# A gated graph network and a batch-normed one: z ahead of the high part, x's load on ScalarE's queue, and row sums of one adjacency on ScalarE

## The chip, the cores and the metric

The kernel runs on one core of a Trainium2 chip. The time is the device time of one execution in microseconds, and lower is better. A comparison of two kernels rests on several executions of each on the same chip. The engines are named as in the profile: PE multiplies matrices (PEld loads its weights), DVE is the vector engine, ACT the scalar engine, POOL the general one (GpSimd), and SP issues most of the transfers. Each engine works through its own instructions in order.

## The reference

There are 16 graphs of 1024 nodes with 128 features, and a dense adjacency of 1024 x 1024 for each, of zeros and ones. The first part runs four gated steps on the normalised features of each graph:

```python
h = relu(layernorm(x))
for i in range(4):
    m  = einsum('bjn,bjd->bnd', adj, h @ weight[i])
    r  = sigmoid(m @ w_ih_r.T + h @ w_hh_r.T + b_r)
    z  = sigmoid(m @ w_ih_z.T + h @ w_hh_z.T + b_z)
    n  = tanh(m @ w_ih_n.T + b_in + r * (h @ w_hh_n.T + b_hn))
    h  = (1 - z) * n + z * h
x = x + h * mask
```

The second part runs four graph convolutions with a batch norm over all graphs and nodes after each:

```python
h = relu(layernorm(x))
for i in range(4):
    h = relu(einsum('bnm,bmc->bnc', adj, h @ W[i]) + b[i])
    h = gamma[i] * (h - mean(h)) * rsqrt(var(h) + 1e-5) + beta[i]
out = x + h
```

## The kernel before, in words

The function that runs is exact_path. It keeps features transposed, 128 features on the partitions and nodes along the row, in two halves of 512 nodes. For the big product with the adjacency the features are split into a high part, which is the value rounded to the short float type fp32r, and a low part, which is what is left. Each adjacency goes through eight row tiles of 128 x 1024, so one aggregation is 8 rows x 2 parts x 2 halves = 32 products of 128x512, all at line 524. Both parts are cast on chip: ACT writes the high part (line 925, method high), DVE subtracts for the low part (line 932, method low).

In the gated part two streams run against each other, sa with the even graphs and sb with the odd ones. A half step (function half_step) puts the gates of one stream, called two, beside the preparation and the aggregation of the other, called one. A counter, clock, begins at 3 and counts them: two first steps, then 60 half steps. The gates of a half are six products at line 999 (method products; each is two PE instructions of 128x512), into four banks named g_r, g_hn, g_xn and g_z. The second half's products use the same four banks, so each of them waits until the first half's reader of that bank is done: the sigmoids at lines 1017 (reset_gate) and 1026 (update_gate, for z) on ACT, and two DVE operations at lines 1018 and 1019. Then come tanh (line 1022, candidate), h minus candidate (line 1035, less), the product with z (line 1039) and the sum with the candidate (line 1040), the last two both in method mixed.

The new h reaches the other layout by way of memory. DVE transposes blocks of it (line 720), SP writes it to cross_h (line 591) and reads it back as n_h (line 598), from which high and low are made one half step later. The aggregation of stream one, which follows the gates on PE, needs high and low of the first half when it starts and those of the second half midway. When it ends, ACT copies its two banks to m (line 961), and the next half step's products begin.

The order of all this is written out by hand for every engine (manual_schedule). Work that recurs only in some half steps is put in an agenda: at(n, place, go) asks that go be issued in half step n at a place such as "start", "beside0", "beside1", "mid", "gap" or "late", and due(place) issues it. A stream's method plan, called with n when the stream begins a graph, puts there the norm of the graph that it finished (sums in "gap" of n+2, stores of xmid and ymid by POOL in "mid", y_mid blocks on ACT in n+4) and the preparation of the graph that it takes next: the load of its x (next_load, line 539, on POOL's queue, "late" of n+4), its sums on DVE, its factors, and its blocks on ACT. For adjacencies, POOL also casts rows to bf16 (line 615), SP transposes them by DMA, and POOL stores the turned adjacency of 2 MB to memory (line 629) for the second part. While a stream is at its last gates, its next adjacency is fetched to stage tiles, rounded on POOL (line 577), and inspected by ACT (glance, line 586), which reads a row tile of 128x1024 into a junk tile and adds it up per partition.

The second part is ordered by a planner, on ACT and DVE from the last gates on. For each graph it loads the turned adjacency (line 1319), casts it to fp32r on DVE and ACT (lines 1324 and 1322), and aggregates. At layer 0 the features come ready from memory (first_split, lines 1379 to 1382, tiles y and chw), and the weights are applied after (first_weights, lines 1391 and 1392). The first graph of later layers is aggregated before its batch norm is known, and raw_weights (line 1409) corrects it with degree, the sums of the first adjacency for each node, kept alike on all partitions. Function row_sums makes them: sixteen products of 128x512 with a matrix of ones (line 1418), and two copies on ACT (line 1422), after the first graph's aggregation of layer 0. PE's order there is the planner's too: they come out in the middle of the second graph's products. degree shares its room with w_mT, the gates' weights, which are then no longer used.

Of the kernel before, what the change touches and what calls it, by code (L numbers as in the profile page):

```python
# [8 lines left out]
F32 = mybir.dt.float32  # L9
# [7 lines left out]
P = 128  # L17
# [324 lines left out]
def exact_path(  # L342
# [39 lines left out]
    def tmp(name):  # L382
        return ps_t.tile([P, HALF], F32, tag="tmp", name=name)

    adjT_d = [dram.tile([NB, P, N], BF16, tag=f"adjT{b}", name=f"adjT_d{b}") for b in range(B)]
    xmid_d = [dram.tile([N, C], F32, tag=f"xmid{b}", name=f"xmid_d{b}") for b in range(B)]
    ymid_d = [dram.tile([P, N], F32, tag=f"ymid{b}", name=f"ymid_d{b}") for b in range(B)]
# [20 lines left out]
    nc.vector.memset(eps_t, EPS)  # L408
    ones = const.tile([P, 1], F32, tag="ones", name="ones")
    nc.vector.memset(ones, 1.0)  # L410
    low = const.tile([P, (B + 2) * NB], F32, tag="low", name="low")
    nc.vector.memset(low, 0.0)

# [119 lines left out]
    with ExitStack() as st:  # L533
# [46 lines left out]
        def glance(b, stage, js):  # L580

            junk = work.tile([P, N], BF16, tag="junk", name=f"junk{b}_{js[0]}", bufs=1)
            for j in js:
                lows = stage[j % 4].bitcast(U16).rearrange("p (n t) -> p n t", t=2)[:, :, 0]
                k = b * NB + j
                nc.scalar.activation(junk, lows, AF.Copy, accum_out=low[:, k : k + 1])

        def exchange_out(t, name, d=None):
            if d is None:
# [180 lines left out]
        class Stream:  # L770
# [35 lines left out]
                norm_blocks(self.xt, self.y, self.norm, ks)  # L806

            def next_load(self):
                self.next_x = load_x(self.b + 2, nc.gpsimd)

            def next_sums(self):
                self.next_norm = norm_stats(self.next_x, f"in{self.b + 2}")
# [12 lines left out]
            def plan(self, n, tail=None):  # L825

                if tail:
                    b, xt, hT, parts = tail
                    end = {}

                    def sums():
                        end["norm"] = tail_sums(b, xt, hT, parts)

                    def blocks(hf):
                        if hf == 0:
                            end["y"] = y_mid(b)
                        norm_blocks(xt, end["y"], end["norm"], range(hf * BH, (hf + 1) * BH))

                    at(n + 2, "gap", sums)
                    at(n + 3, "mid", lambda: store_xmid(b, xt))  # L840
                    at(n + 3, "gap", lambda: norm_factors(end["norm"]))
                    at(n + 4, "beside0", lambda: blocks(0))
                    at(n + 4, "beside1", lambda: blocks(1))
                    at(n + 5, "mid", lambda: store_ymid(b, end["y"]))
                if self.b + 2 < B:
                    at(n + 4, "late", self.next_load)
                    at(n + 6, "start", self.next_sums)
                    at(n + 6, "gap", self.next_factors)
# [123 lines left out]
            def gate_step(self, hf, between=None):  # L972
                self.products(hf)
                self.reset_gate(hf)
                if between:
                    between()
                self.candidate(hf)
                self.update_gate(hf)
                self.less(hf)
                self.mixed(hf)  # L980

            def products(self, hf):
# [47 lines left out]
            def less(self, hf):  # L1030
# [3 lines left out]
                else:  # L1034
                    nc.vector.tensor_sub(ho, hin, self.r)  # L1035

            def mixed(self, hf):
                ho = self.now[2]
                nc.vector.tensor_mul(ho, ho, self.z)  # L1039
                self.last_dve = nc.vector.tensor_add(ho, ho, self.r)  # L1040
                if hf == NH - 1:
                    self.hT = self.new
                    self.i += 1
# [28 lines left out]
        def first_step(one, two, gated, halfway):  # L1072

            feed.next_step()
            if one is sa:
                feed.jobs = transposes([(s.b, s.rows) for s in (sa, sb)])
            one.split_step()
            feed.some(2)
            two.gate_step(0)
            two.half_away(0)  # L1080
            if feed.full or (clock[0], "mid") in agenda:
                mids(two)
            feed.some(1)
            two.gate_step(1)
            two.half_away(1)
            due("late")
            gated()
            one.agg_step(0)
            halfway()
            feed.some(NB if one is sa else 1)  # L1090
            one.agg_step(1)
            two.finish()
            clock[0] += 1
# [8 lines left out]
        def half_step(one, two, gated=None, halfway=None):  # L1102
# [22 lines left out]
            two.fetch_more()  # L1125
            two.candidate(0)
            two.less(0)
            one.high(0)
            two.update_gate(0)
            one.low(0)  # L1130
            two.mixed(0)
            two.half_away(0)
            two.first_four()
            if feed.full or (clock[0], "mid") in agenda:
                mids(two)
            one.high(1)
            feed.some(counts[1])
            two.products(1)
            two.reset_gate(1)
            due("beside1")  # L1140
            two.first_glances()
            due("late")
            one.low(1)
            two.candidate(1)
            two.less(1)
            two.update_gate(1)
            two.last_four()
            two.mixed(1)
            two.half_away(1)
            due("outs")  # L1150
            due("gap")
            due("end")
            if gated:
                gated()
            one.agg_step(0)
            if halfway:
                halfway()
# [8 lines left out]
        with tc.manual_schedule(engines=every):  # L1166
# [115 lines left out]

            sa.plan(0)
            sb.plan(1)
            first_step(sa, sb, looks, lambda: ahead(1))
            first_step(sb, sa, lambda: turn_ih(prep, w_g, 2), lambda: ahead(2))
            written[0] = False
# [122 lines left out]
            nc.tensor.matmul(pc[hf], w_c[:, i, :], mt[:, cols], start=True, stop=True)  # L1410
        conv_done(0, i, pc, stats)

    def row_sums(rows):

        pd = [tmp(f"pt_deg{hf}") for hf in range(NH)]
        for j in range(NB):
            for hf in range(NH):
                nc.tensor.matmul(
                    pd[hf], ones_r, rows[j][:, hf * HALF : (hf + 1) * HALF], start=(j == 0), stop=(j == NB - 1)
                )  # L1420
        for hf in range(NH):
            nc.scalar.copy(degree[:, hf * HALF : (hf + 1) * HALF], pd[hf])

    xo = []

    def pieces(b):
# [28 lines left out]
            for n0, n in pieces(k):  # L1455
                nc.gpsimd.dma_start(xo_piece(k, n0, n), by_node(xmid_d[k], n0, n))

    ones_r = work.tile([P, P], F32R, tag="ones_r", name="ones_r", bufs=1)
    nc.vector.tensor_copy(ones_r, ones.to_broadcast([P, P]))
    degree = w_mT.rearrange("p l c -> p (l c)")[:, :N]  # L1460

    stats = small.tile([P, B * NH, 6], F32, tag="bn_st", name="stats0")
# [1 line left out]
    for b in range(B):  # L1464
        rows = load_adjT(b, 0)
        hw_next = first_split(b + 1) if b + 1 < B else None
        pm = banks(b, 0)
        aggregate(pm, hw, rows, 0)
        if waiting:
            last = first_weights(*waiting, stats)  # L1470
            if b == 1:
                with tc.issue_after(last.ins):
                    sb.rest()
        if b == B - 1:
            hw_next = raw_split(1)
# [118 lines left out]
```

## Time and profile before

| what | value |
|---|---|
| median of three runs | 1773.89 us |
| the three runs | 1771.36, 1773.89, 1773.9 us |
| the profiled execution, its own time | 1774.21 us |
| its span, first to last instruction | 1772.3 us |
| mean granted PE clock | 0.998 |
| DMA: read from memory, written to it | 267.47 MB, 97.52 MB |

Times in the profile are counted in microseconds from the start of the span. A row of a timeline gives the start, the length, the engine, the line, the operation, the tile written and the tiles read, their shapes and the number of instructions merged in the row; behind it, in brackets, stands how long the engine sat idle before and what ended that. A row of waits gives who waited for whom, the total, how many times, and the longest. Names carry an engine and a line: "PE g_z L999 <- ACT z L1026" is PE's product into bank g_z at line 999, waiting for ACT's instruction that writes z at line 1026. "SPq" is SP issuing a transfer; the transfer lands later. Products on PE are pipelined, so a busy row of 1.02 us for two instructions is followed by the next pair 0.86 us after its start; a loss on PE is read from starts, not from busy time.

### The profile page before, as it was taken

How to read it: one execution, taken by the hardware profiler on the slowest of the kernel's cores; microseconds unless marked ns; L12 is line 12 of the kernel's file. 1: busy time of each engine (PE TensorE's matmuls, PEld its weight loads, DVE VectorE, ACT ScalarE, POOL GpSimd, SP SyncE). 2: the span in 40 equal slices, each digit the busy share in tenths (PEclk: the TensorE clock that was granted, in tenths of full speed). 3: DMA queues.
4: the chain of work that ended last, by engine and by line, in shares of the span. 5: the costliest groups of instructions: out<-in, count | busy, mean ns of one | idle time of the engine just before them, and what ended most of it. 6: DMA issues, size and time to landing. Idle time of an engine off the chain costs nothing. (4 is left out here: it accounts for less than half of the span.)

```text
span 1772.3 us, 22314 instructions
## 1 busy us (share of the span) xinstructions
PE 1754.2 (99%) x6734; PEld 1194.8 (67%) x6734; DVE 1288.6 (73%) x2310; ACT 1108.6 (63%) x1713; POOL 373.0 (21%) x415
## 2 busy tenths in 40 slices
PE   9999999999999999999999999999999999999997
PEld 6565656565656565656565656577778888888886
DVE  7676867877777887877787786766666666666665
ACT  5356556556556556655755654486777767767765
POOL 4224223332332331422422323010100000000010
PEclk9999999999999999999999999999999999999999
DMA  7558578677677776766866858788866676757667
GB/s 256 144 155 290 141 204 282 169 214 242 209 204 221 227 202 209 253 194 204 270 182 169 309 147 229 281 280 293 292 228 215 226 249 205 251 211 255 232 221 268
DMA packets 363618, 400.16 MB, mean 226 GB/s; under 512 B 158189, under 2 KB 239889, under 8 KB 363489
## 3 DMA queue, kind: packets, MB, share of 16 engines
q1 hardware_dynamic: 342736, 323.59, 58.5%
q0 software_dynamic: 20224, 74.80, 11.8%
q8 instruction: 55, 0.90, 0.2%
q14 instruction: 75, 0.61, 0.1%
q10 hardware_dynamic: 528, 0.26, 0.0%
HBM read 267.47 MB, written 97.52 MB: 206 GB/s over the span
## 5 line engine op out<-in xcount | busy, mean ns | idle before, releaser
L524 PE MATMUL pm<-row,ghw 128*128 128x512 f32 x2048 | 503.5, 403 | 0.1
L524 PEld LDWEIGHTS pm<-row,ghw 128*128 128x128 f32 x2048 | 384.1, 188 | 105.5 <-issue 29.1
L524 PE MATMUL pc_m<-wide,chw 128*128 128x512 f32 x1024 | 245.3, 395 | 0.0
L615 POOL CAST half<-row 128x1024 bf16<-128x1024 f32 x128 | 141.9, 1120 | 397.8 <-DMA adjT<-half 384.6
L524 PEld LDWEIGHTS pc_m<-wide,chw 128*128 128x128 f32 x1024 | 190.5, 188 | 41.8 <-issue 3.8
L961 ACT COPY m<-pm 128x512 f32<-128x512 f32 x128 | 68.7, 588 | 207.4 <-PE pm L524 207.4
L1018 DVE SCALAR_TENSOR_TENSOR r<-g_hn,vecs,r 128x512 f32<-128x512 f32 x128 | 93.6, 731 | 136.9 <-ACT r L1017 75.5
L1022 ACT ACTIVATE r<-r,vecs 128x512 f32<-128x512 f32 x128 | 92.4, 722 | 158.4 <-DVE r L1019 156.4
L524 PE MATMUL pc_g_r<-wide,chw 128*128 128x512 f32 x464 | 187.1, 403 | 0.3 <-ACT chw L501 0.3
L524 PE MATMUL pc_g_z<-wide,chw 128*128 128x512 f32 x464 | 181.2, 391 | 0.0
L577 POOL CAST row<-stage 128x1024 fp32r<-128x1024 f32 x112 | 128.4, 1154 | 203.7 <-DMA stage<-in_adj_dram 169.1
L1324 DVE CAST wide<-block 128x1024 fp32r<-128x1024 bf16 x160 | 110.0, 692 | 75.4 <-PE pc_m L524 44.7
L1324 DVE CAST wide<-packed 128x1024 fp32r<-128x1024 bf16 x160 | 110.3, 692 | 71.9 <-PE pc_g_z L524 54.1
L1322 ACT CAST wide<-packed 128x1024 fp32r<-128x1024 bf16 x96 | 100.6, 1048 | 58.5 <-PE pc_m L524 28.3
L1322 ACT CAST wide<-block 128x1024 fp32r<-128x1024 bf16 x96 | 100.7, 1049 | 53.7 <-PE pc_g_z L524 27.7
L999 PE MATMUL g_r<-m,w_mT 128*128 128x512 f32 x256 | 130.8, 592 | 0.3 <-ACT m L961 0.3
L999 PE MATMUL g_xn<-m,w_mT 128*128 128x512 f32 x256 | 130.8, 593 | 0.0
L999 PE MATMUL g_z<-m,w_mT 128*128 128x512 f32 x256 | 130.8, 592 | 0.0
L1372 DVE BATCH_NORM_STATS2 stats<-feat 128x6 f32<-128x512 f32 x128 | 84.1, 686 | 47.0 <-ACT feat L1371 45.9
L1017 ACT ACTIVATE r<-g_r,brz 128x512 f32<-128x512 f32 x128 | 87.9, 686 | 41.7 <-PE g_r L999 41.2
L1035 DVE TENSOR_TENSOR h<-h,r 128x512 f32<-128x512 f32 x96 | 83.3, 868 | 41.7 <-ACT r L1022 41.7
L1039 DVE TENSOR_TENSOR h<-h,z 128x512 f32<-128x512 f32 x128 | 106.7, 834 | 6.8 <-ACT z L1026 0.2
(186 smaller groups left out, 2817.9 us busy)
## 6 DMA issues: line engine op xcount, KB each, us to landing
block<-adjT_d SPq DMA_DIRECT2D x256, 256.0 KB, 4.8
packed<-adjT_d SPq DMA_DIRECT2D x256, 256.0 KB, 5.5
stage<-in_adj_dram SPq DMA_DIRECT2D x120, 512.0 KB, 5.4
adjT_d<-adjT POOLq DMA_DIRECT2D x16, 2048.0 KB, 8.1
cross_h<-t_h SPq DMA_DIRECT2D x92, 256.0 KB, 2.2
n_h<-cross_h SPq DMA_DIRECT2D x368, 64.0 KB, 2.1
xmid_d<-x POOLq DMA_DIRECT2D x16, 512.0 KB, 6.3
y<-ymid_d POOLq DMA_DIRECT2D x16, 512.0 KB, 5.3
```

Source lines behind the costliest of these rows:

```text
L524: nc.tensor.matmul(pm[hf], hw[s][:, j * P : (j + 1) * P], rows[j][:, hf * HALF : (hf + 1) * HALF], start=(j == 0 and s == 0), stop=(j == N ...
L577: nc.gpsimd.tensor_copy(t, stage[j % 4])
L615: nc.gpsimd.tensor_copy(t, row.bitcast(F32))
L999: nc.tensor.matmul(po, wT[:, i, g * C : (g + 1) * C], rhs, start=start, stop=stop)
L1017: nc.scalar.activation(r, pr, AF.Sigmoid, bias=brz[:, 3 * i : 3 * i + 1])
L1018: nc.vector.scalar_tensor_tensor(r, phn, b_hn(i), r, ALU.add, ALU.mult)
L1022: nc.scalar.activation(self.r, self.r, AF.Tanh, bias=b_in(self.i))
L1035: nc.vector.tensor_sub(ho, hin, self.r)
L1039: nc.vector.tensor_mul(ho, ho, self.z)
L1322: nc.scalar.copy(r, t)
L1324: nc.vector.tensor_copy(r, t)
L1372: nc.vector.bn_stats(stats[:, b * NH + hf, :], dst)
```

## The change

There are three parts.

In half_step the product of h with z gets a method of its own, scaled, out of mixed. For the first half, z's sigmoid and that product are issued ahead of the high part, and then high, low and the rest of mixed follow. The high part of the second half is issued after that half's products and reset gate, where before it came ahead of them. In gate_step nothing changes in order.

The load of the next graph's x is issued by ACT in "beside0" of half step n+5, where POOL issued it in "late" of n+4, and its sums are asked for in "gap" of n+5, where it was "start" of n+6. The place "late" goes, and gated, which turns weights in a first half step, is called ahead of "gap".

The row sums are taken by ACT from the rows of sa's first adjacency, in eight places of half steps 5 to 8, with the accumulating copy that glance uses. The eight columns are written to memory by POOL in "mid" of half step 9, and read back to all partitions by POOL in the second part, at the third graph of layer 0. The sixteen products, their ones and their two copies go. The products added up the columns of the turned adjacency, which are the rows of the adjacency itself, so both ways give the same sums.

```diff
+    degree_d = dram.tile([N], F32, tag="degree", name="degree_d")
...
+    by_row = const.tile([P, NB], F32, tag="by_row", name="by_row")
...
+        def row_sums(rows, js):
+
+            for j in js:
+                junk = work.tile([P, N], BF16, tag="junk", name=f"summed{j}", bufs=1)
+                nc.scalar.activation(junk, rows[j].bitcast(F32), AF.Copy, accum_out=by_row[:, j : j + 1])
...
             def next_load(self):
-                self.next_x = load_x(self.b + 2, nc.gpsimd)
+                self.next_x = load_x(self.b + 2, nc.scalar)
...
                 if self.b + 2 < B:
-                    at(n + 4, "late", self.next_load)
-                    at(n + 6, "start", self.next_sums)
+                    at(n + 5, "beside0", self.next_load)
+                    at(n + 5, "gap", self.next_sums)
                     at(n + 6, "gap", self.next_factors)
...
                 self.less(hf)
+                self.scaled()
                 self.mixed(hf)
...
+            def scaled(self):
+                ho = self.now[2]
+                nc.vector.tensor_mul(ho, ho, self.z)
+
             def mixed(self, hf):
                 ho = self.now[2]
-                nc.vector.tensor_mul(ho, ho, self.z)
                 self.last_dve = nc.vector.tensor_add(ho, ho, self.r)
...
             two.candidate(0)
             two.less(0)
+            two.update_gate(0)
+            two.scaled()
             one.high(0)
-            two.update_gate(0)
             one.low(0)
             two.mixed(0)
             two.half_away(0)
             two.first_four()
             if feed.full or (clock[0], "mid") in agenda:
                 mids(two)
-            one.high(1)
             feed.some(counts[1])
             two.products(1)
             two.reset_gate(1)
+            one.high(1)
             due("beside1")
             two.first_glances()
-            due("late")
             one.low(1)
             two.candidate(1)
             two.less(1)
             two.update_gate(1)
             two.last_four()
+            two.scaled()
             two.mixed(1)
             two.half_away(1)
             due("outs")
+            if gated:
+                gated()
             due("gap")
             due("end")
-            if gated:
-                gated()
             one.agg_step(0)
...
+            for n, place, js in (
+                (5, "beside1", (0,)),
+                (6, "beside0", (1,)),
+                (6, "beside1", (2,)),
+                (6, "gap", (3,)),
+                (7, "gap", (4, 5, 6)),
+                (8, "start", (7,)),
+            ):
+                at(n, place, lambda js=js: row_sums(sa.rows, js))
+            at(9, "mid", lambda: nc.gpsimd.dma_start(degree_d.rearrange("(j p) -> p j", p=P), by_row))
...
-    def row_sums(rows):
-
-        pd = [tmp(f"pt_deg{hf}") for hf in range(NH)]
-        for j in range(NB):
-            for hf in range(NH):
-                nc.tensor.matmul(
-                    pd[hf], ones_r, rows[j][:, hf * HALF : (hf + 1) * HALF], start=(j == 0), stop=(j == NB - 1)
-                )
-        for hf in range(NH):
-            nc.scalar.copy(degree[:, hf * HALF : (hf + 1) * HALF], pd[hf])
...
-    ones_r = work.tile([P, P], F32R, tag="ones_r", name="ones_r", bufs=1)
-    nc.vector.tensor_copy(ones_r, ones.to_broadcast([P, P]))
...
-        if b == 0:
-            row_sums(rows)
+        if b == 2:
+            nc.gpsimd.dma_start(degree, degree_d.partition_broadcast(P))
```

More of the change, by code (lines that the diff above doesn't have):

```diff
@@ L1139, in half_step @@
             two.reset_gate(1)
+            one.high(1)
             due("beside1")
             two.first_glances()
-            due("late")
             one.low(1)
```

## The prediction

> **What bounds the kernel now.** I read the first lines of the page, then what PE waits for, then PE's timeline, and only there the other engines.
>
> ```profile
> span 1772.3 us, 22314 instructions
> PE 1754.2 (99%) x6734; PEld 1194.8 (67%) x6734; DVE 1288.6 (73%) x2310; ACT 1108.6 (63%) x1713; POOL 373.0 (21%) x415
> PEclk9999999999999999999999999999999999999999
> ```
> PE is never out of work for long and its clock is granted in full, so time goes only with PE work or PE's gaps. DVE, ACT and POOL have slack on the whole; what matters is where one of them is late for PE. PE's own waits:
>
> ```profile
> PE g_z L999 <- ACT z L1026: 3.6, 4, 1.8
> ```
> That is nearly all the mid-kernel idle time. The largest, in PE's timeline:
>
> ```profile
> 230.50 1.02 PE L999 MATMUL g_xn<-m,w_mT 128*128 128x512 f32 x2
> 233.35 1.12 PE L999 MATMUL g_z<-h,w_hhT 128*128 128x512 f32 x2 [1.83 <-ACT z L1026]
> 234.31 1.02 PE L999 MATMUL g_z<-m,w_mT 128*128 128x512 f32 x2
> ```
> Pairs start 0.86 us apart elsewhere; here 2.85 and 0.96, so 2.09 us are lost. ACT in the same stretch:
>
> ```profile
> 225.12 0.69 ACT L1017 ACTIVATE r<-g_r,brz 128x512 f32<-128x512 f32 x1
> 225.71 1.64 ACT L680 ACTIVATE y_mid<-x,ms_mid,rs_mid 128x128 f32<-128x128 f32 x4
> 227.43 0.72 ACT L1022 ACTIVATE r<-r,vecs 128x512 f32<-128x512 f32 x1
> 232.09 0.62 ACT L925 CAST ghw<-n_h 128x512 fp32r<-128x512 f32 x1 [3.94 <-DMA n_h<-cross_h]
> 232.62 0.68 ACT L1026 ACTIVATE z<-g_z,brz 128x512 f32<-128x512 f32 x1
> 234.31 0.62 ACT L925 CAST ghw<-n_h 128x512 fp32r<-128x512 f32 x1 [1.01 <-DMA n_h<-cross_h]
> ```
> The high part waits 3.94 us for the fetched h, z stands behind it, and z frees the bank that PE needs. Why the fetch is late, POOL's timeline and then SP's:
>
> ```profile
> 218.30 0.89 POOL L629 DMA_DIRECT2D adjT_d<-adjT  x1 [2.97 <-DMA adjT<-half]
> 219.18 0.89 POOL L752 DMA_DIRECT2D xmid_d<-x  x1
> 220.06 0.89 POOL L539 DMA_DIRECT2D x<-in_x_dram  x1
> ```
> ```profile
> 221.75 0.34 SPq L591 DMA_DIRECT2D cross_h<-t_h  x1
> 222.20 10.49 SPq L598 DMA_DIRECT2D n_h<-cross_h  x8
> ```
> Three POOL transfers, 3 MB, stand in front. The x load lands at 231.2, SP's cross_h at 230.9 (9.2 us after its issue, where 2.2 is the median), the first half's n_h at up to 231.9.
>
> **Part 1, z ahead of the high part.** Besides 233.35 the same pattern loses 0.71 us at 89.17, 0.36 at 374.33, 0.96 at 515.87 (start-to-start as above): 4.12 in all. (A fifth z wait, at 29.56, is in the first gate step, whose order stays.) New order on ACT at 228: tanh to 228.15, z by 228.8, against 231.36 when PE wants the bank: the wait goes. Late next is the low part, which the aggregation reads. High still starts with the landing, 232.09, low ends 233.43 (as before plus nothing, since less and the z product are done by then); PE, unstalled, wants it after two more pairs, 231.36+1.72=233.08. So 0.0 to 0.4 of the 2.09 come back, depending on the landing. At 515.87 low ends 515.96 for 516.7, at 374.33 it ends 374.4 for 375.8, at 89.17 at 89.25 for 90.2: nothing returns there. At 95.34 PE waits 0.33 for w_both behind the same chain, and 0 to 0.3 is lost more. Gain 3.4 to 4.1.
>
> Price in the other 56 half steps: low stands behind one more DVE product (0.69; up to 1.52 beside a POOL cast), high behind z (0.58 step). Low normally ends 6.5 to 6.8 us into a step whose aggregation starts at 9.9; the tightest step (347.9) ends low at 9.0, after a 1.52 us low, with 0.98 to spare. Minus 0.69 that leaves 0.3, so 0; at most a second slow product (0.83) makes 0.5 in some six such steps, 0 to 3, I take 0.2. High for half 1 moves behind reset's sigmoid, 0.6 later, but its low part waits on DVE's chain (high done at 6.8 to 8, low at 10.6 to 13): nothing. The four instructions are only moved.
>
> **Part 2, coming x on ScalarE.** POOL drops 14 issues of 0.89 us; its next casts start earlier, which nobody waits for. ACT gains 14 issues. The one ACT issue on record (512 descriptors of x) took 0.43; SP's like rows run 0.38 to 1.67, once 4.01. Behind it on ACT stand y_mid, tanh, z. In steps like 222.7 z ends about 228.8+0.5 against 231.36; in sb's steps ACT idles 1.82 before tanh. I take 0.43 each, hidden; without cover 14 x 0.43 = 6. The load moves behind the row of POOL's stores: x, 512 KB, at the 257 GB/s of 226 to 231, is 2.0 us that no longer stand ahead of n_h; if it shares the engines evenly, about half. The fetch lands 0 to 2 us earlier in sa's seven steps, worth 0 to 0.4 (only Part 1's remainder). In sb's seven steps the load now meets n_h head on, up to 2 us later, against margins of 2.5 to 3.4 at low: 0. The sums read x at the step's end, 14 us after the issue, against 11.2 for the longest landing; their DVE position is the same (nothing else lies between "gap" and the next "start").
>
> The trace's packets show none of SP's queue from 219 to 226 while POOL's store ran: a queue can starve another. The Trainium skill (DMA: Bandwidth & Descriptors, Queues, rings and completion order) says engines take turns between queues packet by packet, and its section Issuing engines are not separate DMA queues says another issuer saves only issue time; this stretch does not show even turns. By that rule alone the fetch would not come earlier, and 0.4 of Part 1 would be missing.
>
> **Part 3, row sums.** Sixteen matmuls leave PE's queue:
>
> ```profile
> 1163.12 0.39 PE L524 MATMUL pc_g_r<-wide,chw 128*128 128x512 f32 x1
> 1163.53 3.91 PE L1418 MATMUL pt_deg<-wide,ones_r 128*128 128x512 f32 x16
> 1167.28 0.39 PE L524 MATMUL pc_g_z<-wide,chw 128*128 128x512 f32 x1
> ```
> 3.75 us from the first to the next product, plus 0.41-0.23=0.18 of a wait ahead (cm on ACT): 3.93. Is the next work ready 3.9 earlier? The casts that waited "PE pt_deg" (1.9 us on ACT and DVE) lose their reason, ACT drops two copies of 0.59. The nearest deadline is chw of the fourth graph, low done 1178.07 for PE at 1182.4: 4.3 spare, and it moves up itself. I take 3.9; lower end 1.0 if ACT's casts hold.
>
> Added: eight ACT sums, 1.17 us each by the glances (84 rows of 1057 ns, 187 ns to read out, overlapped) = 9.4 us, in ACT's gaps: before tanh 1.8 to 3, after z 4 to 6. The tightest is the three in "gap" of the step at 117.3:
>
> ```profile
> 130.18 0.30 ACT L668 ACTIVATE rs_in<-mv_in,eps_t 128x8 f32<-128x8 f32 x1
> 134.87 1.07 ACT L961 COPY m<-pm 128x512 f32<-128x512 f32 x2 [4.39 <-PE pm L524]
> ```
> 3 x 1.17 ends at 134.1, 0.8 before m. The one in "start" delays reset's sigmoid by 1.17 to 139.1, PE wants that bank at 140.06. Sum 0 to 0.5, I take 0. The degree store of 1024 four-byte pieces costs POOL some 0.9 (as x's 1024 rows) plus a pace copy of 0.19, between casts that wait 1.08 for stage at 167.85; its packets are short beside stage's 512 KB. The broadcast load (512 KB) stands where DMA is 0.84 busy; nothing reads it until about 1330. Both 0 (upper end 0.5 each).
>
> **Sum.** 3.9 (Part 3) + 3.75 (the middle of Part 1's gain) - 0.2 (low behind the product) - 0.2 (the small upper ends of Part 3) = 7.25 saved, against the profiled execution's own 1774.21 (span 1772.3 and 1.9 around): 1767.0. That run lies 0.32 above the median of 1773.89, whose lowest run is 1771.36; the z waits hang on landings and may differ between runs. I say **1767.0**, own range 1764.5 to 1769.5.
>
> **Rivals.**
> A: the z wait comes back as a wait for the low part. For it: landings of 232 leave low only 0.35 late even now. Against: three of four places have 0.7 to 1.4 spare. If x's 512-byte packets push n_h 2 us later at all four, Part 1 gives about 0.5: 1774.2-3.9-0.5 = 1769.8.
> B: the row sums' room is not used, because ACT's casts hold PE up (ACT is 82% busy from 1151 to 1180): 1 of 3.9 stays, 1770.1.
> C, slower: ACT stands blocked in the x issue. SP's four n_h issues took 222.20 to 227.7 beside POOL's store, at half x's descriptors. Stuck from 225.8 to 231, tanh, behind y_mid, ends 233.4 and z 234: PE waits 2.7 in each of sa's seven steps, 19 us, in place of 4.1: 1774.2-3.9+14.9 = 1785. It decides from a block of about 4.2 us (2.6 of slack and 1.6 x 7 = 3.5+7.6). Against: ACT's queue is empty, and SP's issue of x took 0.38 in front of a backlog.
> D: all gains small or eaten by the planner's new order in the second half, which it writes itself: 1772 to 1776.
>
> **How the numbers follow.** A measurement of this kernel tells about 0.2%, 3.5 us. Likeliest 0.66; A 0.09; B 0.08; C 0.09; D 0.08. Faster takes the likeliest, A and most of B: 0.81; same D and B's rest: 0.10; slower C: 0.09. The range 1764 to 1771 holds the likeliest, A and B.
>
> **What would show it.** Right: no PE wait for ACT z in half steps; sixteen fewer 128x512 products and first_weights straight behind; steps of 17.57 throughout, but about 18 at 222; ACT's x issues near 0.43. Wrong: PE waiting for ghw before pm, x issues of several us on ACT, or m copies late behind the sums. The forecast falls with C, or if the planner's order opens new gaps after 1151.

## The result, and the profile after

The changed kernel takes 1775.29 us (median of 14 runs, 1773.19 to 1777.48), the kernel before 1771.8 us (median of 14 on the same chip, 1770.22 to 1774.15). The ratio is 1.0015, with a 95% interval of 1.0009 to 1.0022: slower by some 2.7 us, clear of the noise but under the 0.2% that the prediction says a measurement can tell, where 1767.0 and "faster" had been forecast.

The page's first lines, which answer to the first fence of before:

```profile
span 1772.9 us, 22290 instructions
PE 1750.4 (99%) x6718; PEld 1190.0 (67%) x6718; DVE 1286.2 (73%) x2309; ACT 1118.6 (63%) x1727; POOL 365.9 (21%) x404
PEclk9999999999999999999999999999999999999999
```

PE has 16 instructions fewer and 3.8 us less busy time, so the row sums did leave it. The span did not follow: 1772.9 against 1772.3. This execution took 1774.69 us, 0.6 under its kernel's median, while the profiled execution of before took 1774.21, 2.4 above its median.

PE's waits after (who waited for whom, total, times, longest):

```profile
PE g_z L1008 <- ACT z L1035: 3.7, 4, 1.5
PE pw_g_hn L1414 <- ACT cm L1413: 0.8, 1, 0.8
PE pm L526 <- DVE ghw L940: 0.3, 1, 0.3
```

The z wait is still there: four times, 3.7 us, where before had 3.6. In both kernels 0.6 of it is in the first gate step, whose order stays; the rest was to go. The second row is a new wait in the graph convolutions, the third the low part standing a little late. PE's timeline after, at the step that was shown of before, and ACT's:

```profile
229.57 1.02 PE L1008 MATMUL g_xn<-m,w_mT 128*128 128x512 f32 x2
232.14 1.13 PE L1008 MATMUL g_z<-h,w_hhT 128*128 128x512 f32 x2 [1.55 <-ACT z L1035]
233.10 1.02 PE L1008 MATMUL g_z<-m,w_mT 128*128 128x512 f32 x2
```
```profile
224.19 0.69 ACT L1026 ACTIVATE r<-g_r,brz 128x512 f32<-128x512 f32 x1
228.80 0.41 ACTq L541 DMA_DIRECT2D x<-in_x_dram  x1
229.25 1.65 ACT L688 ACTIVATE y_mid<-x,ms_mid,rs_mid 128x128 f32<-128x128 f32 x4 [4.38 <-DMA cross_h<-t_h]
230.81 0.71 ACT L1031 ACTIVATE r<-r,vecs 128x512 f32<-128x512 f32 x1
231.42 0.67 ACT L1035 ACTIVATE z<-g_z,brz 128x512 f32<-128x512 f32 x1
231.99 0.61 ACT L933 CAST ghw<-n_h 128x512 fp32r<-128x512 f32 x1
```

z now stands ahead of the high part, as written. But ACT does nothing from 224.88, where the reset sigmoid ends, to 228.80, where it issues x's load, and what ended its idle time is a transfer of SP's: the store cross_h. That store went out at 223.22 and landed at 228.70. In the trace every transfer has a completion semaphore, a counter that it raises when it lands. The store's is number 101, and x's load on ACT's queue is given number 101 too; ACT's instruction ahead of the issue waits for that semaphore and ends at 228.76, just behind the landing. The issue itself took 0.41 us, as forecast; the wait for it took 3.9. In all five steps with such a wait the load's semaphore was last used by a transfer of SP's, and the issue follows its landing by 0.02 to 0.1 us. ACT's own waits, in which before has no row for cross_h:

```profile
ACT y_mid L688 <- DMA cross_h<-t_h: 14.5, 4, 4.4
ACT r L1031 <- DMA n_h<-cross_h: 4.4, 1, 4.4
```

So in five of sa's seven steps tanh and z stand behind an SP transfer. POOL's timeline and then SP's show what stands ahead of that store:

```profile
218.11 0.89 POOL L637 DMA_DIRECT2D adjT_d<-adjT  x1 [3.05 <-DMA adjT<-half]
218.98 0.89 POOL L760 DMA_DIRECT2D xmid_d<-x  x1
```
```profile
223.22 0.34 SPq L599 DMA_DIRECT2D cross_h<-t_h  x1
223.66 6.36 SPq L606 DMA_DIRECT2D n_h<-cross_h  x7
```

x's load is gone from POOL, so 2.5 MB stand ahead of the fetch and not 3; the store takes 5.5 us from issue to landing, where before took 9.1. It is earlier than before, and still late for ACT. In the convolutions the products of pt_deg are gone, and what comes in their place waits a little for ACT, which itself sat idle until POOL's store of ymid had landed:

```profile
1165.67 1.13 PE L1414 MATMUL pw_g_hn<-cm,w_c 128*128 128x512 f32 x2 [0.80 <-ACT cm L1413]
```
```profile
1165.03 1.08 ACT L1413 COPY cm<-pc_m 128x512 f32<-128x512 f32 x2 [1.25 <-DMA ymid_d<-y_mid]
```

There is a second difference, which no wait shows. The DMA view of before, then of after (a queue's packets, MB and share of 16 engines; then an issue's count and median us to landing):

```profile
q1 hardware_dynamic: 342736, 323.59, 58.5%
adjT<-half SPq DMA_TRANSPOSE x128, 2.8
out_dram<-w_hhT SPq DMA_DIRECT2D x3, 256.0 KB, 2.3
```
```profile
q1 hardware_dynamic: 342736, 323.59, 60.9%
adjT<-half SPq DMA_TRANSPOSE x128, 3.3
out_dram<-w_hhT SPq DMA_DIRECT2D x3, 256.0 KB, 2.6
```

SP's queue q1 carries the same packets and the same bytes, and needs 2.4 points more of the engines' time. Transposes that nothing in the change touches land 0.5 us later, and so do output stores at the other end of the kernel, by 0.3.

By stages (step 6 begins with the first m copy of the half step at 80; 59 steps of 17.57 would be 1036.6 us; the convolutions run from the m copy of the last step to the first product of the output transposes):

| profiled execution | to step 6 | 59 half steps | convolutions | from there to the end | span |
|---|---|---|---|---|---|
| before | 80.0 | 1043.2 | 620.5 | 28.5 | 1772.3 |
| after | 79.8 | 1043.9 | 617.9 | 31.3 | 1772.9 |
| only1 | 79.2 | 1038.9 | 620.5 | 28.4 | 1767.1 |
| pad32 | 80.1 | 1068.3 | 620.5 | 29.3 | 1798.2 |
| after256 | 79.4 | 1039.0 | 616.6 | 30.3 | 1765.3 |
| after_behind | 80.2 | 1040.2 | 617.8 | 30.4 | 1768.6 |

The last four rows are experiments, told below. The changed kernel wins 2.7 us in the convolutions, loses 0.7 in the half steps, where 3.75 were to be won, and loses 2.8 at the end.

### The profile page after: what moved, and what is told of

It reads as the page before. It is cut to its first block, busy times and chain, and to the rows that moved or that the text cites. A ratio compares the mean times of both kernels' runs of the same rounds, so it can differ in the third digit from the quotient of the medians.

```text
span 1772.9 us, 22290 instructions
## 1 busy us (share of the span) xinstructions
PE 1750.4 (99%) x6718; PEld 1190.0 (67%) x6718; DVE 1286.2 (73%) x2309; ACT 1118.6 (63%) x1727; POOL 365.9 (21%) x404
## 5 line engine op out<-in xcount | busy, mean ns | idle before, releaser
L1344 ACT CAST wide<-packed 128x1024 fp32r<-128x1024 bf16 x96 | 100.6, 1048 | 57.3 <-PE pc_m L526 30.3
L1044 DVE TENSOR_TENSOR h<-h,r 128x512 f32<-128x512 f32 x96 | 77.0, 802 | 73.3 <-ACT r L1031 73.3
```

Of the source, the lines that this page charges most:

```text
L1344: nc.scalar.copy(r, t)
```

## The experiments

All are timed in five rounds against the kernel before on the same chip; a ratio is to that, with its 95% interval. One per mille is 1.8 us.

### The parts one by one

**no2** is the changed kernel without the second part:

```diff
-                self.next_x = load_x(self.b + 2, nc.scalar)
+                self.next_x = load_x(self.b + 2, nc.gpsimd)
...
-                    at(n + 5, "beside0", self.next_load)
-                    at(n + 5, "gap", self.next_sums)
+                    at(n + 4, "late", self.next_load)
+                    at(n + 6, "start", self.next_sums)
...
```

> The changed kernel with its second part undone: x's load is back on POOL's queue in "late" of n+4, its sums in "start" of n+6; z ahead of the high part and the row sums on ACT stay. Theory (ACT stands blocked at x's issue until an SP transfer has landed, and that is where the gain went): z comes by 6.1 to 8.4 us into every step, no g_z wait is left in steps of about 80, 222, 365, 506; 3.6 us fewer of PE products; 1767 to 1769.5 us against 1771.8 of the kernel before, so at least 4 us under the changed kernel's 1775.3. Rival 1 (the loss lies in the new order of high, low and the z product, or in the row sums): it stays within 1.5 us of the changed kernel, 1774 or more. Rival 2 (the final stores hold the end, and an earlier PE is worth nothing): 1771 to 1772, with a longer tail behind the last PE product.

**only1** is before with the first part alone:

```diff
             two.less(0)
+            two.update_gate(0)
+            two.scaled()
             one.high(0)
-            two.update_gate(0)
             one.low(0)
...
```

> The kernel before with only z and its product put ahead of the high part (and the second half's high behind that half's reset gate). Theory: the z waits of the profile before (4.1 us there, in typical executions perhaps 2, since that one ran 2.4 over the median of 14) go, and nothing else: 1768.5 to 1770.5 against 1771.8. Rival 1 (the order itself costs, low standing behind the product on DVE): 1773 or more, with PE waiting for ghw of DVE before pm. Rival 2 (wait moves on to low, or the end is held by the stores): 1771 to 1772.5.

**only2** is before with x's load and sums moved as in the change:

```diff
-                self.next_x = load_x(self.b + 2, nc.gpsimd)
+                self.next_x = load_x(self.b + 2, nc.scalar)
...
```

> The kernel before with only x's load moved to ACT's queue in "beside0" of n+5 and its sums to "gap". Theory (the issue blocks ACT, with y_mid, tanh, high and z behind it): slower than before by 3 to 8 us, 1775 to 1780; in the first stream's seven steps x's issue comes 5 to 7 us into the step in place of 2.4, and z behind it even later than in the changed kernel, since here high stands ahead of z. Rival 1 (the loss is in the new order or the row sums): 1771 to 1772.5, as before. Rival 2 (it does what it was said to do, the fetch comes earlier): 1769 to 1771.

**only3** is before with the row sums on ACT, and the sixteen products gone:

```diff
+    by_row = const.tile([P, NB], F32, tag="by_row", name="by_row")
...
-        if b == 0:
-            row_sums(rows)
+        if b == 2:
+            nc.gpsimd.dma_start(degree, degree_d.partition_broadcast(P))
...
```

> The kernel before with only the row sums taken by ACT in steps 5 to 8, and degree stored and read back; the sixteen products go. Theory: PE has 3.63 us less to do and about 2.5 of it arrives at the last PE product; 1768.5 to 1770 against 1771.8. Rival 1 (ACT's sums, the store of 1024 pieces or the broadcast load cost as much as the products): 1771.5 to 1774. Rival 2 (the end is held by the output stores): PE ends 2.5 earlier but the span does not, 1771 to 1772.

| kernel | median us | before | ratio |
|---|---|---|---|
| only1 | 1769.69 | 1771.56 | 0.9987 (0.9978 to 0.9996) |
| only2 | 1773.21 | 1771.56 | 1.0012 (1.0003 to 1.0021) |
| only3 | 1803.0 | 1771.56 | 1.0163 (1.0140 to 1.0187) |
| no2 | 1785.65 | 1771.56 | 1.0083 (1.0069 to 1.0096) |

only1 came out as the theory had it. only2 lies between theory and rival: the second part costs 2.1 us alone. The other two fell outside everything that was expected: without the second part, which I held to be the culprit, the changed kernel is 12 us worse (1.0083 against 1.0015) and not 4 better, and the third part alone costs 29 us (0.0163 of 1771.6), which no expectation had foreseen. Its row sums run from 93 to 138 us, yet PE's waits for z are long in all of sa's steps up to 966:

```profile
PE g_z L1007 <- ACT z L1034: 24.1, 9, 4.6
```

It has only two transfers of degree, at 170 and 1146 us, yet the transposes take 3.3 us in the median. Something that holds for the whole program had changed.

### One tile of 32 bytes

by_row, eight values of four bytes per partition, is laid out ahead of low, and all tiles come one behind the other. By the program's own layout x begins, in the kernel before, at byte 35328 of each partition, which is 138 x 256, and the tiles that transfers use in these stages (x, t_h and n_h, adjT, the bf16 rows half, the rows, h) all begin at a multiple of 256. Behind by_row they begin 32 bytes off one. **pad32** adds that much to the kernel before and nothing else:

```diff
+    pad = const.tile([P, NB], F32, tag="pad", name="pad")
+    nc.vector.memset(pad, 0.0)
     low = const.tile([P, (B + 2) * NB], F32, tag="low", name="low")
```

> The kernel before with one more tile of 32 bytes per partition (set to zero, never read) ahead of the tile low, which is where the row sums' tile by_row stands in the changed kernel; nothing else. The program lays its tiles out one behind the other, so all later tiles, those that transfers read and write among them, move by 32 bytes; in the kernel before they begin at multiples of 256. Theory (where the transfers' tiles begin decides how fast the transfers go): it is slower by 15 to 35 us, 1787 to 1806, with the transposed rows landing in 3.3 us in place of 2.8, z waits of 2 to 5 us in the first stream's seven steps, and the output stores slower. Rival 1 (the row sums' own work, their store of 1024 four-byte pieces or the tile in memory is what cost only3 its 31 us): 1771 to 1772.5, as before.

**after64**, **after128** and **after256** are the changed kernel with by_row made larger, here the last:

```diff
-    by_row = const.tile([P, NB], F32, tag="by_row", name="by_row")
+    by_row = const.tile([P, 8 * NB], F32, tag="by_row", name="by_row")
...
```

> The changed kernel with by_row taking 64 bytes in place of 32, so that later tiles move by 64 bytes against the kernel before. Theory A (64 is enough): 1764 to 1768, transposed rows land in 2.8 us. Theory B (it takes a multiple of 256, as in the kernel before): about as the changed kernel, 1773 to 1777, rows land in some 3.3. Rival (places don't matter): 1775.

> The changed kernel with by_row taking 256 bytes, so that every later tile begins at a multiple of 256 bytes as in the kernel before. Theory (the places of the tiles took the gain): 1764 to 1768 against 1771.6 of the kernel before, close to the 1767 forecast; no z wait over 0.5 us in half steps, x's issues on ACT at 2 to 3 us into the step. Rival 1 (places don't matter, ACT's blocked issue costs by itself): 1773 to 1776. Rival 2 (both): 1769 to 1772.

> The changed kernel with by_row taking 128 bytes, so that later tiles begin 128 bytes off a multiple of 256. Moves of 32 and 64 bytes measured 1775.3 and 1776.3, of 256 bytes 1766.7. Theory A (128 is enough): 1766 to 1768, isolated transposes 2.7 us, the store's packets 159 ns. Theory B (it takes 256): 1774 to 1777, transposes 3.2 us, packets near 171 ns.

**no2_256** is no2 with the larger tile.

> As after256, but with x's load back on POOL in its old place: the first and third parts of the change without the second. Theory: 1766 to 1769, since the first part alone measured -1.9 us and the third takes 3.6 us off PE, of which some 2.5 reach the end; the second part is then worth -1 to +3 us by the difference to after256. Rival (the row sums' own work costs): 1771 or more, in spite of the places.

| kernel | tiles moved by | median us | before | ratio |
|---|---|---|---|---|
| pad32 | 32 | 1803.68 | 1771.39 | 1.0185 (1.0168 to 1.0203) |
| changed kernel | 32 | 1775.29 | 1771.8 | 1.0015 (1.0009 to 1.0022) |
| after64 | 64 | 1776.25 | 1771.39 | 1.0027 (1.0017 to 1.0038) |
| after128 | 128 | 1775.62 | 1773.44 | 1.0015 (1.0006 to 1.0024) |
| after256 | 256 | 1766.69 | 1771.39 | 0.9971 (0.9959 to 0.9982) |
| no2_256 | 256 | 1767.5 | 1771.39 | 0.9975 (0.9966 to 0.9984) |

Thirty-two bytes that nobody reads cost 32 us. Moves of 64 and of 128 bytes are no better than 32; at 256 the change is worth 5.1 us (by its interval 3.2 to 7.3), and 1766.69 is what had been forecast. PE's largest waits and the DMA view of pad32:

```profile
PE g_z L1001 <- ACT z L1028: 22.6, 9, 4.4
PE pt_idle L1175 <- POOL ident masks.py:199: 2.4, 1, 2.4
```
```profile
q1 hardware_dynamic: 342736, 323.59, 59.7%
q0 software_dynamic: 20224, 74.80, 12.3%
adjT<-half SPq DMA_TRANSPOSE x128, 3.3
```

The kernel is the one before, and the wait that took 3.6 us there takes 22.6: the fetch comes late in every step of sa's that has POOL's burst of transfers. (The three longest waits, of 3.7, 4.4 and 4.3 us, cost PE more than themselves: in the clock records the granted clock falls to 0.5 for 3.4 us at 236.3, 383.0 and 816.5, around the end of each, and those steps lose 1.8 to 2.0 us beyond the wait. So the mean granted clock is 0.996 where before had 0.998.) The queues' shares rise from 58.5 and 11.8 for the same bytes; in after256 q1's is back:

```profile
q1 hardware_dynamic: 342736, 323.59, 58.4%
adjT<-half SPq DMA_TRANSPOSE x128, 3.1
```

The second of these rows shows that the transposes' median landing mixes two things: it is 3.1 in after256 and 3.4 in only2, both with their tiles in place but with x's load on ACT's queue beside the transposes. In the packet records of POOL's queue, its 4096-byte packets have a median of 171 ns in pad32, 159 in before, 171 in after64 and after128, and 159 in after256. Transposes with no other kind of transfer under way tell the tiles' part alone: 2.74 us in before, 2.73 in after256, 3.23 in pad32, 3.2 in after64 and after128. The engines' own instructions take in pad32 what they took in before (PE's products 592 ns, DVE's low parts 684 in the median), so it is the transfers that the places slow.

The Trainium skill (DMA: Bandwidth & Descriptors, How a descriptor splits into AXI transactions) says that a descriptor is carried out in transactions that must start at multiples of 256 bytes, so that one which starts elsewhere begins with a transaction from the multiple below. The step between 128 and 256 agrees with that; by its count, an estimate, 4096 bytes make 17 transactions for 16, which would be 6%, and the packets here took 7.5% longer. The packets of 512 bytes don't agree: by the same count they would make 3 for 2, and their median is 27 ns in before and in pad32. The same page's DMA Transpose section, under Constraints, asks 32-byte alignment of a transpose; these transposes ran at 32 bytes off, 0.5 us slower.

### Which tiles

**shift_adjT** moves the tile adjT alone, by a pad of 32 bytes ahead of it and one of 224 behind, so that the rest stays at multiples of 256; **shift_half** does so with the two bf16 rows that the transposes read; **shift_x** with the small tiles, x, and the tiles of t_h and n_h (the weights lie among the small tiles and move with them). The first:

```diff
+            pad_a = keep.tile([P, 8], F32, tag="pad_a", name="pad_a")
+            nc.vector.memset(pad_a, 0.0)
             stage = keep.tile([P, NB, N], BF16, tag="adjT", name="stage", bufs=1).bitcast(F32)
+            pad_b = keep.tile([P, 56], F32, tag="pad_b", name="pad_b")
+            nc.vector.memset(pad_b, 0.0)
```

> The kernel before with a tile of 32 bytes ahead of the tile adjT and one of 224 behind it (both set to zero, never read): adjT alone, which the transposed rows are written to and the 2 MB stores are read from, begins 32 bytes off a multiple of 256; tiles behind it are back on one. In pad32 the isolated transposes took 3.2 us in place of 2.7, and the store's packets 171 ns in place of 159; isolated n_h and cross_h transfers were as long as before. Theory A (adjT's place is what pad32 paid for): 1790 to 1804 against 1771.5, transposes at 3.2 us. Theory B (the rows that the transposes read, tiles half): 1771 to 1773 here. Theory C (x, t_h and n_h): 1771 to 1773 here.

> The kernel before with the two bf16 row tiles, which the transposes read, alone moved by 32 bytes (32 ahead of them, 224 behind). Theory A (adjT): 1771 to 1773, transposes at 2.8 us. Theory B (half): 1785 to 1804, transposes at 3.2 us, the store's packets still 159 ns.

> The kernel before with 32 bytes ahead of the tile low and 224 ahead of adjT: the small tiles, the four x tiles and the eight tiles that t_h and n_h share move by 32 bytes, adjT and all behind it stay at multiples of 256. Theory A (adjT) and B (half): 1771 to 1773. Theory C (x, t_h, n_h): 1785 to 1804, with n_h landing later in the first stream's seven steps although transposes stay at 2.8 us.

| kernel | median us | before | ratio | worth |
|---|---|---|---|---|
| shift_adjT | 1775.3 | 1772.62 | 1.0018 (1.0008 to 1.0028) | 3.2 us |
| shift_half | 1784.36 | 1772.62 | 1.0069 (1.0056 to 1.0082) | 12.2 us |
| shift_x | 1787.14 | 1772.62 | 1.0084 (1.0071 to 1.0097) | 14.9 us |

Each theory had one place pay for everything; in fact all three places pay. The three sum to 30.3 of pad32's 32.8 us; the rows and h, which move in pad32 too, weren't tried alone. Each has its own mark: with adjT moved only POOL's packets are long (168 ns), transposes alone take 2.73 us; with half moved the transposes alone take 3.22 and the packets 159. With x, t_h and n_h moved, isolated fetches are hardly longer (2.00 us against 1.96), so their 15 us must come where transfers meet, which no run shows directly; which of the three tiles pays wasn't tried. A part in each is the clock, which fell to 0.5 for 3.4 us once with adjT moved and twice each with half and with x.

### Controls, and the third part by itself

**only3_256** is only3 with by_row at 256 bytes; **pad256** is before with a pad of 256 bytes; **dram4k** is before with only the 4 KB tile degree in memory, written once at the start:

```diff
+    degree_d = dram.tile([N], F32, tag="degree", name="degree_d")
...
     nc.vector.memset(low, 0.0)
+    nc.gpsimd.dma_start(degree_d.rearrange("(p j) -> p j", p=P), low[:, :NB])
```

> The third part alone as in only3, but with by_row taking 256 bytes, so that all tiles stay at multiples of 256. Theory (the sums themselves cost nothing, the places did): 1768 to 1769.5, which is 1771.5 less the 2 to 3 us that 16 products leave at PE's last product; with the first part's -1.9 that sums to the 1767.5 of no2_256. Rival (the two parts overlap): 1767 to 1768 or 1770 to 1772.

> The kernel before with a tile of 256 bytes per partition where pad32 had 32 bytes: all later tiles move, and every one still begins at a multiple of 256. It is the control of the move itself. Theory: 1771 to 1773, as before. Rival (any move of the small tiles costs, which would explain that only3_256 gained nothing): 1773.5 or more.

> The kernel before with the 4 KB tile degree in memory ahead of the others and one short store of zeros to it by POOL at the start (nothing reads it), so that xmid, ymid and the exchange tiles in memory move by 4 KB as in the changed kernel. only3_256 measured no gain although PE lost 3.63 us of work. Theory A (its z waits were as in the kernel before, which alone swing by some 5 us from run to run): 1771 to 1773 here. Theory B (the move in memory slows the fetch and takes the third part's gain): 1773.5 to 1776.

only3_256 took 1773.83 against 1772.62, a ratio of 1.0001 (0.9993 to 1.0010); pad256 1773.16 against 1773.44, 1.0001 (0.9992 to 1.0010); dram4k 1773.08 against 1773.44, 1.0003 (0.9993 to 1.0013). So neither the move by 256 nor the move in memory costs anything. The third part alone still returns nothing: its convolutions take 617.9 us where before took 620.5, but its half steps 1045.4 where before took 1043.2, with z waits that cost 2.1 us at 232 and 1.2 at 1079, and a wait of 1.2 for the low part at 943. On top of the first part, which takes the z waits away, it seems to pay: 0.9987 becomes 0.9975, 2.1 us, though the two intervals overlap. Why sa's fetch should be later with the row sums is open; its eleven times run from 1769.58 to 1777.11.

### ACT's wait at x's issue

**after_behind** is the changed kernel, tiles 32 bytes off, with x's issue behind z:

```diff
-                    at(n + 5, "beside0", self.next_load)
+                    at(n + 5, "late", self.next_load)
...
             two.scaled()
+            due("late")
             one.high(0)
```

> The changed kernel, places of its tiles as they are, with the issue of x's load on ACT moved behind z's sigmoid of the first half, where it can hold up neither tanh nor z. Theory (ACT stands at that issue until an SP transfer has landed, and the z waits of 1.82, 1.39, 0.72 and 0.33 us in the changed kernel's profile are that): those four go, z ends by 6.1 us in all steps with the load, and some of it comes back as waits for the low part, which depends on the fetch alone: 1771.5 to 1773.5 against 1775.3. Rival (z came late only because the tiles' places delay everything): 1774.5 to 1776.5.

It took 1770.79 us against 1773.44, a ratio of 0.9985 (0.9976 to 0.9994), where the changed kernel had 1.0015: 5.3 us, more than expected. ACT's timeline in the same step:

```profile
224.36 0.69 ACT L1026 ACTIVATE r<-g_r,brz 128x512 f32<-128x512 f32 x1
224.95 1.64 ACT L688 ACTIVATE y_mid<-x,ms_mid,rs_mid 128x128 f32<-128x128 f32 x4
226.66 0.72 ACT L1031 ACTIVATE r<-r,vecs 128x512 f32<-128x512 f32 x1
227.42 0.69 ACT L1035 ACTIVATE z<-g_z,brz 128x512 f32<-128x512 f32 x1
230.05 0.38 ACTq L541 DMA_DIRECT2D x<-in_x_dram  x1
230.55 0.62 ACT L933 CAST ghw<-n_h 128x512 fp32r<-128x512 f32 x1 [2.44 <-DMA n_h<-cross_h]
```

ACT still stands at the issue for 1.9 us, but nothing that PE needs is behind it except the high part, which waits for the fetch anyway. No half step with the load then has a z wait; step 222 lasts 17.57 us, where the changed kernel's took 19.99.

**after256_behind** has both amendments.

> Both amendments: by_row takes 256 bytes, and the issue of x's load on ACT stands behind z's sigmoid. after256 measured a ratio of 0.9971 to the kernel before, with z at 8.5 us and 0.06 us lost in one step where x's issue came 5.2 us into it. Theory (with the tiles at multiples of 256 the block at x's issue is short enough to be hidden): 0.9965 to 0.9975, no difference that can be told from after256. Rival (the block still costs): 0.996 or less. Other rival (x later means more trouble for n_h and the transposes): 0.998 or more.

It took 1767.66 against 1773.12, a ratio of 0.9967 (0.9955 to 0.9980), which can't be told from after256. With the tiles at multiples of 256, the store lands earlier (3.2 us after its issue in the step at 222, where the changed kernel's took 5.5) and the wait is short enough. after256's ACT in that step:

```profile
223.71 0.69 ACT L1026 ACTIVATE r<-g_r,brz 128x512 f32<-128x512 f32 x1
224.95 0.41 ACTq L541 DMA_DIRECT2D x<-in_x_dram  x1
225.40 1.65 ACT L688 ACTIVATE y_mid<-x,ms_mid,rs_mid 128x128 f32<-128x128 f32 x4 [1.00 <-DVE r L1027]
227.57 0.67 ACT L1035 ACTIVATE z<-g_z,brz 128x512 f32<-128x512 f32 x1
```
```profile
ACT y_mid L688 <- DMA cross_h<-t_h: 5.6, 3, 2.6
PE g_z L1008 <- ACT z L1035: 0.6, 1, 0.6
```

z begins at 227.57 in place of 231.42. Its only PE wait for z is the one of the first gate step, whose order never changed. after256, after256_behind and no2_256 can't be told apart; they are the fastest kernels of this study, ahead of both that it began with.

## Why the prediction was wrong, point by point

**The step that failed** is Part 3's list of what is added. It priced eight sums, a store and a load, and gave nothing to the tile that holds the sums. That tile moves every later tile 32 bytes off a multiple of 256. In the changed kernel this is worth 0.0044 of the time, 7.8 us (after against after256), about the 8.3 by which the forecast missed. In the kernel before it is worth 32. Most of the 7.8 goes by way of ACT's wait at x's issue, the step that failed in Part 2: with that moved (after_behind against after256_behind) the tiles' places are worth 3.2 us, and with the tiles in place moving it is worth nothing that can be told.

**Part 3, the products.** "3.93 on PE" was 3.63 by instructions (16 x 0.227), and the convolutions became shorter by 2.7 in the changed kernel, 3.1 in no2_256 and 3.9 in after256. I took 3.9 with a lower end of 1.0 if ACT's casts hold (rival B). At the one new wait of PE's they don't hold it up: ahead of pw_g_hn's 0.8 us for cm in the changed kernel, ACT is idle for 1.25 us until POOL's store of ymid has landed, 4.9 us after its issue, where after256's landed in 3.6 and PE didn't wait. The eight sums in ACT's gaps, costed at nothing, delayed nothing by more than 0.2 us in after256. Behind the convolutions 2.8 us are lost again (31.3 against 28.5). Output stores land later there (2.6 us for 2.3), but that doesn't explain it: after256, whose stores are as fast as before, takes 30.3, and pad256, which differs from before by an unused tile alone, 29.3. This stays open.

**Part 1.** The waits for z go where nothing else holds z: in only1 the half steps take 1038.9 us, 4.3 less than before, against 3.4 to 4.1 forecast. Low behind one more product cost next to nothing: one late step in only1, 0.2 us. By the ratio only1 gains 2.3 us (0.7 to 3.9), less than 3.75, though the interval doesn't exclude it. The term was right for the execution in the profile, whose 1774.21 us lay 2.4 above the median of 14; with three runs known I had put that difference at 0.32. Typical executions seem to have fewer z waits to give: dram4k and pad256, which do nearly the same work as before, show 2.0 and 2.4 us of them in half steps, where before showed 3.0.

**Part 2.** "I take 0.43 each, hidden" has the issue right, 0.41 us, and the cover wrong: ACT stands up to 4.0 us ahead of the issue, and y_mid, tanh and z with it. This is rival C's effect at C's place, for another reason: C had the issue itself take long beside a backlog. C was given 0.09 because "ACT's queue is empty"; the queue was, but ACT waited for a landing on SP's, through a completion semaphore that both use. C's arithmetic held: with 2.6 us of slack and a stand of 4.4, PE should wait 1.8, and it lost 1.71 between the starts 229.57 and 232.14. Four of sa's steps paid and not seven: two had no such stand, and in the one at 80, with 4.0 us the longest, z still began 7.7 us into the step, where the four have it at 8.1 to 9.6. The other half of Part 2, the fetch that no longer waits behind x, was right and undervalued: with the tiles off, no2's first fetch lands 12.5 us into that step and the changed kernel's 8.1, and the second part turns 1.0083 into 1.0015. With the tiles mended it is worth 0.7 us, inside what can be told.

**Rivals.** A (low takes z's place) shows in no2, where PE waits 7.6 us for the high part in five half steps, for z in none:

```profile
PE pm L526 <- ACT ghw L933: 7.6, 5, 2.9
```

In the changed kernel it is the 0.3 us of pm. D's outcome, 1772 to 1776, holds the measured time, but mostly not for D's reason: the convolutions, which the planner orders, did become shorter. Only for the 2.8 us behind them, which stay open, can D not be excluded.

**The number.** With the places kept, after256 measured 1766.69 and the forecast was 1767.0. Part of that is luck: the gain was 5.1 us by the ratio where 7.25 had been summed, and the base lay 2.4 too high.

## What to carry to other kernels

A new tile costs at least its place: look at what is laid out behind it, and keep the tiles that transfers use at multiples of 256 bytes, as a 32-byte tile cost this kernel 32 us. In a profile this shows as transfers that the change doesn't touch taking longer for the same bytes, so compare the DMA view's shares, and transfers that have the queues to themselves, before reading waits. Issue a transfer from an engine only where nothing urgent stands behind it, since the issue can wait for another queue's landing; and make the sum against the median of many runs, not the profiled one.

## What the runs showed of the hardware that I had not expected

- Tiles 32, 64 or 128 bytes off a multiple of 256 slow transfers: POOL's 4096-byte packets took 171 ns against 159, a lone transpose 3.2 us against 2.74. Lone fetches of 512-byte packets hardly changed (27 ns a packet, about 2.0 us).
- In this program a load issued by ACT waited up to 4.0 us for the landing of a transfer issued by SP, because the two were given the same completion semaphore (101 in the step shown, where the wait was 3.9).
- A placement effect of 32 us in one order of work (pad32) is 19 in another (no2 against no2_256, with z ahead of the high part) and 8 in a third (after against after256, with x's load on ACT too), where the slower transfers are mostly hidden.
- A wait of PE's of some 2 us or more can cost more than itself: in pad32, only3, no2 and the shifted kernels the granted clock fell to 0.5 for 3.4 us around waits of 2.0 to 4.6 us, 14 times in all, and stayed at 1.0 through others as long (2.8 us in pad32, 3.7 in only3).
